# Dealing a graph layer's projections out between its neighbour sums

## The chip, the core and the metric

The kernel runs on one NeuronCore of a Trainium2 chip. The core has five engines with instruction queues of their own, each worked off in order: TensorE (PE, matmuls; PEld its weight loads), VectorE (DVE), ScalarE (ACT), GpSimd (POOL) and SyncE (SP, which here only issues transfers). Matmuls write to PSUM, a small memory of eight banks. The metric is device microseconds of one execution; the time before is the median of three runs.

## The reference

A graph of 6250 nodes with 256 features and 100,000 edges, sorted by their target node, each edge with one of 8 relations. Two relational graph layers run after a layer norm, then a layer norm and a mixture of 8 experts of which each node takes two. Cut to what matters:

```python
def _rgcn_conv(x, W, Wroot, b, src, dst, etype):
    seg = dst * R + etype
    sums = segment_sum(x[src], seg)              # per node and relation
    cnt = segment_sum(ones, seg)
    mean = (sums / maximum(cnt, 1)).reshape(N, R, -1)
    return x @ Wroot + b + einsum('nrd,rde->ne', mean, W)

h = relu(_rgcn_conv(layernorm(x), W1, Wroot1, b1, ...))
x = x + _rgcn_conv(h, W2, Wroot2, b2, ...)
# experts: logits = xf @ Wg + bg; the two largest, softmax;
# out += w[e] * (gelu(xf @ W1[e] + b1[e]) @ W2[e] + b2[e]); x = x + out
```

## The kernel before

Edges come in 782 tiles of 128. A tile's source rows are fetched by one indirect gather on POOL (L680) from the table `xs`, which holds each row as three bf16 parts; DVE builds a one-hot tile `oh` of target and relation (L686); TensorE multiplies the two, 2 chunks by 3 parts, into a PSUM tile of sums `pg` (L696), and in layer 1 adds a matmul with `ones16` that counts the edges (L699). There are 13 buffers `ge` for gathered tiles.

`_plan` puts the tiles into 194 groups of 1 to 6. Each group has one `pg` tile of which there are two; ACT zeroes it ahead of the sums (L672, in `tiles_in`) and DVE adds it into one of two rings in SBUF at an offset read from a register (L710, in `add`). Groups are walked from both ends of the sorted edges, "up" and "down", one ring for each; the two meet in one block (`join`).

Nodes come in 49 blocks of 128. A block is *whole* at the step after which no further group adds to it; `_plan` works that step out from a margin over the expected edge positions. From there its work is due at fixed distances in steps: `counts`, `invert` (1 / count), `project`, `clear`, `finish`, `turn`, `logits`. `project` makes the block's output: the root term and 8 relations, 2 chunks each, 18 fp32 matmuls in five PSUM tiles `pr` of two terms each (L783), which DVE scales by the inverse counts and adds up in `h` (L791, L793). `clear` zeroes the block's ring rows on ACT (L800). `finish` writes the block out: in layer 1 as three bf16 parts to the table of layer 2, in layer 2 to the output and, normalised, to `xnd`. `turn` transposes it on TensorE, and `logits` makes the gating logits of layer 2 and, once four blocks have them, calls `choose` (the two experts of each node, with a PSUM tile `rpp`); `append` writes the lists of nodes by expert (PSUM tile `rpl`).

In PSUM, `pg` has three banks a tile in layer 1 and two in layer 2. `pr`, the transposes, the counts and the logits share two tiles under the tag "mm"; choosing and lists have two of their own in layer 2 under the tag "rt".

The order within an engine is not the order of the program text: a planner places the instructions by priority and its own estimate of when each is ready, so text that is next to each other may come out mixed. Bounds worked out by `_plan` are tested against the data in the kernel; if one failed, a slower general arm would run.

After the layers the experts run in tiles of 256 rows: gather, two fp32 matmul stages, and a scatter that adds to the output.

Of the kernel before, what the change touches and what calls it, by code (L numbers as in the profile page):

```python
# [48 lines left out]
P = 128  # L49
# [45 lines left out]
Z = 4.8  # L95
WIN = 64
RB = 3
READ = 2
TAKE = 3
EARLY = 30  # L100

# [1 line left out]
def _plan(N, E, R):  # L103

    T = -(-E // P)

    def windows(ts, n):

        mid = n // 2
        lo, hi = [0] * n, [-(1 << 30)] * n
        for t in ts:
            for k in range(n + 1):
                i0, i1 = t * P, max(0, t + k - mid) * P
                mean = N * (i1 * i1 - i0 * i0) / (E * E)
                sd = 2 * N * i0 / (E * E) * math.sqrt(abs(i1 - i0)) + 0.004 * abs(mean)
                if k < n:
                    lo[k] = min(lo[k] if t != ts[0] else 1 << 30, math.floor(mean - Z * sd) - (k < mid))
                if k:  # L120
                    hi[k - 1] = max(hi[k - 1], math.ceil(mean + Z * sd) + (1 if k <= mid else 2))
        shift = -min(lo)
        w = [(a + shift, b + shift) for a, b in zip(lo, hi)]
        return shift, w, max(b for _, b in w)


    NB = -(-N // P)
    mid = max(0, round((N / 4 - P / 2) / P))
    split = round(T * math.sqrt((mid + 0.5) * P / N))
    regions = []  # L130
    t = 0
    while t < T:
        left = (split if t < split else T) - t
        for n in range(min(6, left), 0, -1):
            ng = max(1, min(36, left) // n)
            shift, w, width = windows((t + n // 2, t + n * (ng - 1) + n // 2), n)
            if width <= WIN:
                break
        regions.append((t, n, ng, shift, w, width))
        t += n * ng  # L140
    groups = []
    for r, (t0, n, ng, *_) in enumerate(regions):
        for g in range(ng):
            groups.append((t0 + g * n, n, r))
    NG = len(groups)
    up = [g for g in range(NG) if groups[g][0] < split]
    down = list(range(NG - 1, len(up) - 1, -1))
    size = [sum(groups[g][1] for g in s) for s in (up, down)]
    seq, at, n = [], [0, 0], [0, 0]
    while len(seq) < NG:  # L150

        s = int(n[1] * (size[0] - EARLY) < n[0] * size[1])
        if at[s] == len((up, down)[s]):
            s = 1 - s
        g = (up, down)[s][at[s]]
        seq.append(g)
        at[s] += 1
        n[s] += groups[g][1]
    step = {g: q for q, g in enumerate(seq)}

    whole = []
    for b in range(NB):
        if b == mid:
            whole.append(NG - 1)
            continue
        p = math.sqrt((b + 1 if b < mid else b) * P / N)
        dev = Z * math.sqrt(E * p * (1 - p)) + 1
        t = int(min(E - 1, E * p + dev) // P) if b < mid else int((E * p - dev) // P)
        whole.append(step[next(g for g, (t0, n, _) in enumerate(groups) if t0 + n > t)])


    bounds = []
    for g in range(NG):
        read, taken = ([b for b in range(NB) if whole[b] + n < step[g]] for n in (READ - 1, TAKE))
        if g < len(up):
            bounds.append((sum(b < mid for b in read) or -NB, sum(b < mid for b in taken) + RB))
        else:
            n = sum(b > mid for b in read)
            bounds.append((NB - sum(b > mid for b in taken) - RB, NB - n if n else 2 * NB))
    return T, regions, groups, seq, len(up), mid, whole, bounds  # L180
# [3 lines left out]
def kernel(  # L184
# [451 lines left out]
    with tc.If(go == 1) as cmp:  # L636
        with ExitStack() as arm:
# [18 lines left out]
            def layer(k):  # L656
# [10 lines left out]

                def tiles_in(g):
                    t0, n, r = groups[g]
                    pg = psum.tile([P, nd, R, WIN], F32, name="pg", tag="pg", bufs=2)  # L670
                    wd = regions[r][5]
                    state["zeroed"] = nc.scalar.copy(pg[:, :nd, :, :wd],  # L672
                                                     zeros[:, None, None, :wd].to_broadcast([P, nd, R, wd]))
                    got = []
                    ohs = ap.tile([P, OHW], BF16, name="oh", bufs=3)
                    o0 = 0
                    for t in range(t0, t0 + n):
                        m = P if t < EC else ER
                        ge = ap.tile([P, 3, KD, P], BF16, name="ge", bufs=13)
                        nc.gpsimd.indirect_dma_start(  # L680
                            out=ge[:m].rearrange("p s k d -> p (s k d)"), out_offset=None, in_=xs[k][:, :],
                            in_offset=bass.IndirectOffsetOnAxis(ap=idx[:m, t : t + 1], axis=0))
                        a, b = regions[r][4][t - t0]
                        oh = ohs[:m, o0 : o0 + (b - a) * R].rearrange("p (r d) -> p r d", r=R)
                        o0 += (b - a) * R
                        nc.vector.tensor_scalar(oh, iota16[:m].rearrange("p (r d) -> p r d", r=R)[:, :, a:b],  # L686
                                                rel[:m, t : t + 1], None, op0=OP.is_equal)
                        got.append((ge, oh, m, a, b))
                    state[g] = (pg, got)

                def sums(g):
                    pg, got = state[g]
                    for ge, oh, m, a, b in got:
                        for c in range(KD):
                            for s in range(3):
                                nc.tensor.matmul(pg[:, c, :, a:b], ge[:m, s, c, :], oh, start=False, stop=False,  # L696
                                                 skip_group_check=True)
                        if nd > KD:
                            nc.tensor.matmul(pg[:, KD, :, a:b], ones16[:m], oh, start=False, stop=False,  # L699
                                             skip_group_check=True)  # L700

                def add(g):
                    pg, _ = state.pop(g)
# [59 lines left out]
                def invert(b):  # L763
                    if k == 0:
# [2 lines left out]
                        nc.vector.tensor_scalar(invs[:, b], pc[:, :R], 1.0, None, op0=OP.max)  # L767
                        nc.vector.reciprocal(invs[:, b], invs[:, b])

                def project(b):  # L770

                    n = rows(b)
# [3 lines left out]
                    h = ap.tile([P, D], F32, name="h", bufs=2)  # L776
                    lhs = [(R, [xT[:, c, :n] for c in range(KD)])]
                    lhs += [(r, [ring[:, c, r, s0 : s0 + n] for c in range(KD)]) for r in range(R)]
                    for i in range(0, R + 1, 2):
                        pr = psum.tile([P, 2, D], F32, name="pr", tag="mm", bufs=MM)  # L780
                        for j, (r, chunks) in enumerate(lhs[i : i + 2]):
                            for c in range(KD):
# [5 lines left out]
                        for j, (r, _) in enumerate(lhs[i : i + 2]):  # L788
                            if r == R:
                                extra = bias1 if k == 0 else state.pop(("xb", b))  # L790
                                nc.vector.tensor_tensor(h[:n], pr[:n, j], extra[:n], OP.add)  # L791
                            else:
                                nc.vector.scalar_tensor_tensor(h[:n], pr[:n, j], invs[:n, b, r : r + 1], h[:n],  # L793
                                                               op0=OP.mult, op1=OP.add)
                    state["h", b] = h

                def clear(b):
# [37 lines left out]
                def logits(b):  # L835
                    if k == 1:
                        gate(place[b], state.pop(("t", b)), rows(b))
                        for o, bs in batches[:-1]:
                            if b == bs[-1]:
                                while todo and todo[0][-1] is not todo[-1][-1]:  # L840
                                    batch()
                                c = choose(bs, o, ap, "rt", 2)
                                todo.extend((j, i, False, c) for j, i in enumerate(bs))

                tiles_in(seq[0])
                due = {}
                for b, q in enumerate(whole):
                    for d, f in ((-1, root), (0, counts), (1, invert), (2, project), (2, clear), (2, finish), (3, turn), (4, logits)):
                        due.setdefault(q + d, []).append((f, b))

                todo = []
# [1 line left out]
                def batch():  # L853

                    if todo:
                        append(*todo.pop(0), ap, "rt", 2)

                due.setdefault(joined, []).append((join, mid))

# [3 lines left out]
                            f(b)  # L863

                cleared[:] = [[(-1, ins) for _, ins in c] for c in cleared]
                for q in range(NG + 5):
                    if k == 1 and q == 2:

                        with tc.issue_after(state["zeroed"].ins):
# [4 lines left out]
                    if q == 0 and k == 0:  # L874
                        for c in range(KD + 1):
                            nc.vector.memset(rings[0][:, c], 0.0)
                            nc.scalar.copy(rings[1][:, c], zeros[:, None, 0:1].to_broadcast([P, R, RING + WIN]))
                    run(q, project, clear)
                    run(q, turn)
                    run(q, finish)  # L880
                    if q < NG:
                        sums(seq[q])
                    run(q, invert, logits)
                    if q < NG:
                        add(seq[q])
# [388 lines left out]
```

## Time and profile before

| | us |
|---|---|
| median of three runs | 3025.12 (3022.4 to 3025.45) |
| profiled execution | 3826.98 |
| its span | 3825.1 |
| TensorE busy, mean granted clock | 2804.2, 0.844 |
| POOL, DVE, ACT busy | 1800.2, 1621.8, 1023.8 |
| gathers L680 | 1564 of 966 ns, first at 83.6, last at 2953.1 |
| sums L696, counts L699, projections L783 | 9384, 782, 3528 matmuls |

The profile is of one execution of its own, which here takes 802 us longer than the median of the runs. A line of a group of instructions has the source line, the engine, the operation and the tiles it writes and reads; after a bar its busy time, the mean duration of one and the idle time of the engine just before, with what ended it. In a line of the timeline the first number is the start, the second the duration, and the bracket holds the idle time before and what ended it. A line of waits gives the total, how often, and the longest. "issue" is idle time that ends with nothing which the profile shows.

### The profile page before, as it was taken

To read this page: it belongs to the slowest core of one execution; us is meant where nothing else is said; L and a number is where in the kernel's file an instruction comes from. 1 tells how busy PE (TensorE), PEld (TensorE's weight loads), DVE (VectorE), ACT (ScalarE), POOL (GpSimd) and SP (SyncE) were. 2 spreads that over 40 slices of the span, in tenths; PEclk is the share of its full clock that TensorE was granted. 3 is DMA by queue.
4 is the path that set the end of the run, shared out by engine and by line. 5 is a ranking of instruction groups with operands and counts; after the bars stand their busy time and mean duration, and the time that the engine had idled before them with its cause. 6 is when DMAs were issued, how large, how long until landed. Compare 5 with 4: busy or idle time off the path is not lost.

```text
span 3825.1 us, 52037 instructions
## 1 busy us (share of the span) xinstructions
PE 2804.2 (73%) x18131; PEld 2321.9 (61%) x18131; DVE 1621.8 (42%) x4676; ACT 1023.8 (27%) x1378; POOL 1800.2 (47%) x2109
## 2 busy tenths in 40 slices
PE   5566676766666876566667766776777499999998
PEld 2455565555555655455555655555555388888887
DVE  6444454544444545344554445544445311111111
ACT  6223233322222323122222222221222122222221
POOL 2545555555555554455555555555444033333332
PEclk8678897878888878677888878787878699999999
DMA  6344444444444443444444444444344444344442
GB/s 226 112 116 117 127 127 119 128 118 117 117 119 118 115 117 105 130 121 126 124 127 120 122 126 131 125 124 123 112 116 116 153 119 115 101 115 115 108 112 45
DMA packets 215591, 461.05 MB, mean 121 GB/s; under 512 B 50716, under 2 KB 123222, under 8 KB 215190
## 3 DMA queue, kind: packets, MB, share of 16 engines
q0 software_dynamic: 120384, 334.45, 32.9%
q1 hardware_dynamic: 83724, 112.33, 8.8%
q10 hardware_dynamic: 11210, 10.81, 0.9%
q8 instruction: 149, 2.44, 0.3%
q14 instruction: 124, 1.02, 0.1%
HBM read 412.02 MB, written 46.31 MB: 120 GB/s over the span
## 4 chain that ended last, share of the span: by engine, by line
PE 59%; issue 12%; another core or an unknown queue 11%; DVE 9%; ACT 5%; DMA 3%; POOL 1%; SPq 0%; DVEq 0%; ACTq 0%; POOLq 0%
PE pr L783 21%; PE pg L696 14%; PE ph L1214 10%; PE po L1225 9%; DVE ring L710 3%; ACT pg L672 2%; DVE oh L686 1%; DVE h L793 1%; ACT ring L800 1%; PE pg L699 1%; PE pl L323 1%; POOL ge L680 1%; PE pt L314 1%; DMA ge<-xs,idx 1%
## 5 line engine op out<-in xcount | busy, mean ns | idle before, releaser
L680 POOL DMA_INDIRECT ge<-xs,idx x1564 | 1511.2, 966 | 1425.1 <-PE pg L696 746.8
L696 PE MATMUL pg<-oh,ge 128*128 128x200 bf16 (+24 forms) x9384 | 932.0, 257 | 441.0 <-issue 207.7
L696 PEld LDWEIGHTS <-ge 128*128 128x128 bf16 x9384 | 764.3, 113 | 578.5 <-issue 508.5
L783 PE MATMUL pr<-gw,ring 128*128 128x256 f32 (+1 forms) x3136 | 861.3, 430 | 222.0 <-DVE h L793 104.6
L783 PEld LDWEIGHTS pr<-gw,ring 128*128 128x128 f32 (+1 forms) x3136 | 663.2, 217 | 382.1 <-DVE h L793 126.3
L710 DVE TENSOR_TENSOR ring<-pg,ring 128x1176 f32 (+31 forms) x388 | 457.0, 1178 | 846.1 <-remote 270.6
L672 ACT COPY pg<-zeros 128x1176 f32<-128x1176 f32 (+31 forms) x388 | 380.4, 981 | 981.4 <-DVE ring L710 584.3
L793 DVE SCALAR_TENSOR_TENSOR h<-pr,invs,h 128x256 f32<-128x256 f32 (+1 forms) x784 | 376.9, 481 | 245.3 <-PE pr L783 178.4
L800 ACT COPY ring<-zeros 128x3072 f32<-128x3072 f32 (+1 forms) x98 | 227.8, 2324 | 794.1 <-PE pr L783 674.3
L1214 PE MATMUL ph<-xT,w 128*128 128x256 f32 x1696 | 377.0, 381 | 0.0
L1225 PE MATMUL po<-fw,hT 128*128 x1696 | 374.4, 379 | 0.0
L1225 PEld LDWEIGHTS po<-fw,hT 128*128 128x128 f32 x1696 | 322.2, 190 | 43.8
L1214 PEld LDWEIGHTS ph<-xT,w 128*128 128x128 f32 x1696 | 320.1, 191 | 41.9
L686 DVE TENSOR_SCALAR oh<-iota,rel 128x152 bf16<-128x152 f16 (+25 forms) x1564 | 331.9, 270 | 30.9 <-PE pg L699 16.2
L1215 ACT ACTIVATE hT<-ph,bcol 128x256 f32<-128x256 f32 x424 | 200.4, 473 | 534.6 <-PE ph L1214 534.2
L1230 POOL DMA_INDIRECT out_dram<-fo,ti x106 | 168.7, 1591 | 229.9 <-DVE wt L1199 107.3
L1186 POOL DMA_INDIRECT xg<-xnd,ti x106 | 105.5, 995 | 357.4 <-DMA ti<-tlist 242.3
L699 PE MATMUL pg<-oh,ones 128*128 128x128 bf16 (+24 forms) x782 | 200.2, 256 | 14.2 <-issue 14.1
L1228 DVE TENSOR_TENSOR fo<-po,b2b 128x256 f32<-128x256 f32 x106 | 45.0, 425 | 299.5 <-PE po L1225 291.6
L1209 DVE COPY bcol<-b1c 128x8 f32 x53 | 9.0, 171 | 302.4 <-ACT hT L1215 301.9
L316 ACT COPY tT<-pt 128x256 f32<-128x256 f32 (+1 forms) x98 | 36.2, 370 | 297.9 <-remote 208.6
L699 PEld LDWEIGHTS <-ones 128*128 128x128 bf16 x782 | 87.8, 112 | 23.5 <-issue 19.9
(190 smaller groups left out, 1431.4 us busy)
## 6 DMA issues: line engine op xcount, KB each, us to landing
w<-in_L_ffn_W_dram SPq DMA_DIRECT2D x53, 1024.0 KB
ge<-xs,idx POOLq DMA_INDIRECT x1564
xt<-in_x_dram SPq DMA_DIRECT2D x96, 128.0 KB
xs<-xb SPq DMA_DIRECT2D x8, 1152.0 KB
xs<-hb SPq DMA_DIRECT2D x48, 192.0 KB
fw<-in_L_ffn_W_dram ACTq DMA_DIRECT2D x8, 1024.0 KB
xt<-in_x_dram SPq DMA_DIRECT2D x8, 768.0 KB
out_dram<-h SPq DMA_DIRECT2D x48, 128.0 KB
```

The costliest lines, as they stand in the source:

```text
L672: state["zeroed"] = nc.scalar.copy(pg[:, :nd, :, :wd], zeros[:, None, None, :wd].to_broadcast([P, nd, R, wd]))
L680: nc.gpsimd.indirect_dma_start(out=ge[:m].rearrange("p s k d -> p (s k d)"), out_offset=None, in_=xs[k][:, :], in_offset=bass.IndirectOffs ...
L686: nc.vector.tensor_scalar(oh, iota16[:m].rearrange("p (r d) -> p r d", r=R)[:, :, a:b], rel[:m, t : t + 1], None, op0=OP.is_equal)
L696: nc.tensor.matmul(pg[:, c, :, a:b], ge[:m, s, c, :], oh, start=False, stop=False, skip_group_check=True)
L699: nc.tensor.matmul(pg[:, KD, :, a:b], ones16[:m], oh, start=False, stop=False, skip_group_check=True)
L710: a = nc.vector.tensor_tensor(slot, pg[:, :nd, :, :wd], slot, OP.add).ins
L783: mm = nc.tensor.matmul(pr[:n, j], chunks[c], w[:, c, r, :], start=(c == 0), stop=(c == KD - 1))
L793: nc.vector.scalar_tensor_tensor(h[:n], pr[:n, j], invs[:n, b, r : r + 1], h[:n], op0=OP.mult, op1=OP.add)
L800: ins = nc.scalar.copy(at, zeros[:, None, None, 0:1].to_broadcast([P, nd, R, P]))
L1214: nc.tensor.matmul(ph[:, :TK], w1[:, k, h * P : (h + 1) * P], xT[:, k, :], start=(k == 0), stop=(k == KD - 1))
L1215: nc.scalar.activation(hT[:, h, :], ph[:, :TK], AF.Gelu, bias=bcol[:, h : h + 1], scale=1.0)
L1225: nc.tensor.matmul(po[:, :D], hT[:, k, f * P : (f + 1) * P], rhs, start=(k == 0), stop=(k == KH - 1))
```

## The change

`project` no longer emits its matmuls at once: it appends its five pairs to a list, and `sums` takes one pair from it after each tile; what is left is emitted after the group's sums and before its `add`. Within a step, `turn` and `clear` come first, then `finish`, then `project`. `clear`, `finish`, `turn` and `logits` are due one step later than before. In layer 2 the sums have three PSUM tiles, and choosing and lists take theirs from "mm". The count matmul loads one column of ones in place of 128 and writes one row. In `_plan`, the margin of a block grows from 1 edge to 32 (`P / 4`) and the groups that may run while a block is read are fewer (`READ - 1`, that is 1, becomes 0). That moves two of the 49 blocks by one step each (from step 164 to 165 and from 28 to 29) and changes 21 of the 194 groups' bounds.

```diff
-        dev = Z * math.sqrt(E * p * (1 - p)) + 1
+        dev = Z * math.sqrt(E * p * (1 - p)) + P / 4
...
-        read, taken = ([b for b in range(NB) if whole[b] + n < step[g]] for n in (READ - 1, TAKE))
+        read, taken = ([b for b in range(NB) if whole[b] + n < step[g]] for n in (0, TAKE))
...
-                    pg = psum.tile([P, nd, R, WIN], F32, name="pg", tag="pg", bufs=2)
+                    pg = psum.tile([P, nd, R, WIN], F32, name="pg", tag="pg", bufs=2 + k)
...
-                            nc.tensor.matmul(pg[:, KD, :, a:b], ones16[:m], oh, start=False, stop=False,
+                            nc.tensor.matmul(pg[0:1, KD, :, a:b], ones16[:m, 0:1], oh, start=False, stop=False,
                                              skip_group_check=True)
+                        go_on()
...
+                pairs = []
+
+                def go_on():
+
+                    if pairs:
+                        f, i = pairs.pop(0)
+                        f(i)
+
                 def project(b):
...
-                    for i in range(0, R + 1, 2):
+                    def pair(i):
                         pr = psum.tile([P, 2, D], F32, name="pr", tag="mm", bufs=MM)
...
+                    pairs.extend((pair, i) for i in range(0, R + 1, 2))
                     state["h", b] = h
...
-                                c = choose(bs, o, ap, "rt", 2)
+                                c = choose(bs, o, ap, "mm", 2)
...
-                    for d, f in ((-1, root), (0, counts), (1, invert), (2, project), (2, clear), (2, finish), (3, turn), (4, logits)):
+                    for d, f in ((-1, root), (0, counts), (1, invert), (2, project), (3, clear), (3, finish), (4, turn), (5, logits)):
...
-                        append(*todo.pop(0), ap, "rt", 2)
+                        append(*todo.pop(0), ap, "mm", 2)
...
-                for q in range(NG + 5):
+                for q in range(NG + 6):
...
-                    run(q, project, clear)
-                    run(q, turn)
+                    run(q, turn, clear)
                     run(q, finish)
+                    run(q, project)
                     if q < NG:
                         sums(seq[q])
+                    while pairs:
+                        go_on()
                     run(q, invert, logits)
```

More of the change, by code (lines that the diff above doesn't have):

```diff
@@ L97 @@
 RB = 3
-READ = 2
 TAKE = 3
```

## The prediction

> **What bounds the kernel now.** I first cut the profiled execution into its stages, from start to end: preparation, gathers of layer 1, the turn between the layers, gathers of layer 2, the turn to the experts, the experts.
>
> ```profile
> core 0: us, PE busy (x) PEld busy (x) DVE busy (x) ACT busy (x) POOL busy (x), PEclk, DMA share, GB/s
> 0.00:84.00 84.00, 45.03 (x132) 19.55 (x132) 55.01 (x223) 52.62 (x82) 15.31 (x334) 0.91 0.73 238
> 84.00:1508.00 1424.00, 973.24 (x7303) 802.57 (x7304) 697.67 (x1647) 439.49 (x474) 759.44 (x782) 0.81 0.42 119
> 1508.00:1555.00 47.00, 34.19 (x186) 27.82 (x184) 26.85 (x61) 14.02 (x18) 0.98 (x2) 0.88 0.12 37
> 1555.00:2953.00 1398.00, 953.32 (x6695) 774.38 (x6695) 667.25 (x2170) 301.25 (x361) 749.44 (x781) 0.80 0.44 125
> 2953.00:3057.00 104.00, 47.44 (x247) 36.77 (x248) 39.55 (x166) 17.55 (x24) 8.50 (x9) 0.70 0.42 141
> 3057.00:3826.00 769.00, 750.98 (x3572) 660.83 (x3570) 135.42 (x412) 198.84 (x420) 266.56 (x204) 0.99 0.41 104
> ```
>
> The experts are TensorE alone (751 of 769 us at clock 0.99) and no line of theirs changes. The change lives in the two layers, where no engine is full: TensorE 68% in both, POOL 53%. So I read the timeline at one projection.
>
> ```profile
> 2509.11 6.27 PE L783 MATMUL pr<-gw,ring 128*128 128x256 f32 x20 [2.21 <-DVE h L793]
> 2515.89 3.47 PE L696 MATMUL pg<-oh,ge 128*128 128x208 bf16 x52
> 2516.51 0.95 POOL L680 DMA_INDIRECT ge<-xs,idx  x1 [9.49 <-PE pg L696]
> 2517.76 0.94 POOL L680 DMA_INDIRECT ge<-xs,idx  x1 [0.30 <-issue]
> 2519.01 0.95 POOL L680 DMA_INDIRECT ge<-xs,idx  x1 [0.30 <-PE pg L696]
> ```
>
> Two things are to be seen. Free of waits, gathers start 1.25 us apart (2516.51, 2517.76, 2519.01: 0.95 of work, 0.30 of gap). And a projection in one piece holds TensorE long enough that no gathered tile (13 buffers) is released: POOL stands 9.49 us, then the sums catch up.
>
> The first gives a floor: 782 gathers by 1.25 us is 977 us a layer. The profiled layers take 1424 and 1398, that is 447 + 421 = 868 us above it. The median of the runs shown is 3025.1, against 3827.0 for the profiled execution (span 3825.1 and 1.9 around it). Taking the other stages as profiled (84 + 47 + 104 + 769 + 1.9 = 1006), the runs leave 2019 us for both layers, only 64 above two floors. So nearly all the 868 belongs to the profiled execution, or the floor is lower in runs than I can see. This decides the size of any gain.
>
> Who holds the gathers? Summing POOL's gaps beyond the usual 0.30 us gives 884 us; in 552 of them, TensorE was in a projection (472) or waiting to start one (80): 62%, or 5.6 us for each of 98 blocks. TensorE's own waits (total, times, longest), first two lines layer 1, last two layer 2:
>
> ```profile
> PE pg L696 <- ACT pg L672: 130.4, 49, 15.1
> PE pr L783 <- DVE h L793: 42.2, 18, 5.7
> PE pr L783 <- DVE h L793: 63.0, 26, 8.3
> PE pg L696 <- ACT pg L672: 36.8, 19, 5.2
> ```
>
> **The change, part by part, against 3827.0.**
>
> *Dealing out.* The planner orders the instructions itself, so I compared the two orders. A projection is 18 matmuls (9 terms by 2 chunks; each shows as two in the trace) in five pieces. Blocks whose 18 stand in one run: layer 1 from 23 to 7 of 49, layer 2 from 19 to 21. So many were already dealt by the planner, and net only 14 blocks are newly dealt. TensorE's work is the same; gathered tiles are released earlier. Bound: nothing, to 14 x 9.5 = 133 us (the stand above). I take half of the mean 5.6 us: 14 x 2.8 = -40, since what TensorE owes is still owed. The wait for DVE's h falls with the same blocks: (42.2 + 63.0) x 14/42 = -35 (0 to -105). The wait for invs (54.7 in layer 1) I leave: in both orders the transpose of the counts stands right before the first piece and shares its tiles.
>
> Against it speaks a rule. The rows first, two chains of projections in layer 1 and one of the experts:
>
> ```profile
> 657.80 6.11 PE pr L783 x28
> 756.20 6.50 PE pr L783 x16
> 3082.42 6.91 PE ph L1214 x32
> ```
>
> That is 0.218, 0.406 and 0.216 us each: full and half clock, and the layers' means are 0.81 and 0.80. The Trainium skill (TensorE: Matmul & The Clock Gate, "A second HAM failure mode: psum-queue depth-cycling") says that small idle times between groups which cycle through PSUM make the clock fall back and recover again and again. By the rule, a dense projection cut into pieces would run at half clock: 14 blocks x 36 x 0.19 = +96 us. By the row of POOL's gaps, TensorE is behind when a projection is due, so sums fill the places between pieces and nothing idles: 0. I take 0, and keep +96 as the end.
>
> *Third tile of sums in layer 2.* ACT zeroes a tile when the add two steps earlier has read it; with three tiles it is an add three steps earlier. TensorE's wait there is 36.8 us; I take -30 (0 to -37). Layer 1, with 130.4, keeps two tiles.
>
> *Gating and lists on the projection's tiles.* In layer 2 the two "rt" tiles go. A pair that meets one tile taken waits for two h (2 x 0.48 us). In the new order 2 of 12 choices are closely followed by pieces, and 17 of 48 lists. A choice holds its tile 8.8 us (median, first matmul to last reading). 2 x 8.8 + 17 x 0.97 = 34 at most, 0 at least since the old order also has pieces among lists; I take +15.
>
> *Later steps.* finish, turn, logits and clear come one step later. DMAs and counts of instructions are the same: per block one row of xs or two of out and xnd on SP's queue, not moved past a gather, as POOL has its own queue. Inside a layer the following groups' gathers hide it (5 us of POOL per step of four tiles). At a layer's end, one more block's chain may stand after the last sum: +2 each, +4 (0 to +12). clear on ACT (1.9 and 2.75 us) frees ring rows for adds two steps after the projection, now with one step between; behind it in ACT's queue wait the next zeroing and DVE's add. The order has two zeroed tiles ahead of it in 33 of 49 blocks of layer 1 (31 before), so 0; without that cover 49 x 2.75 = 135 us of TensorE's waits.
>
> *The rest.* The count matmul with one weight column: 782 at the pace of their columns either way (the trace's one-column matmuls of 32 columns start 0.025 us apart, no slower than their neighbours), weight load hidden: 0, at most the whole 88 us of loads if the cover were real work. The plan: two blocks become whole one step later, and the stricter bounds still hold (worked out from the inputs, the least margin is 20 rows, 42 before), so the same arm runs: 0.
>
> Sum: -40 - 35 - 30 + 15 + 4 = -86, so 3741 profiled. For the runs there are two scalings. In proportion, 86/868 of 64 gives -6. Unscaled gives -86, which is more than the 64 that stand above the floor. Waits by order exist in runs too, but count only where gathers run dry; I take a third of the unscaled, -30: **2995**.
>
> **The rivals.**
> - *Hidden anyway.* Gathers pace the runs, and the 13 buffers (16 us of gathers) cover a projection of 8 us at full clock. For it: the 64 us. Time: 3019 to 3031.
> - *More than that.* If a gather's period without the profiler is under 1.25 us, the floor is lower and TensorE's waits count in full: -86 and more, 2940. Against it: the period is sharp, 1.245 to 1.251 us in over half of all gathers.
> - *Slower: the shared tiles.* In layer 2 a list's tile is held 10.9 us (median) in the old order. If the new order keeps that, 48 x 10.9 = 523 of 1398 us leave pairs one tile: 37% of 245 pairs, 92, each 0.97 to 1.5 us: +90 to +138 on TensorE. It decides when TensorE's work and waits pass 977 us: with the profiled busy time of 953 spare is 24, so +66 to +114 and some 3110; at full clock (I work out 655 us from columns and 0.216) spare is 322 and it costs nothing. Between: 3060. Against it: in the new order only 3 matmuls of projections stand between the two matmuls of a list (6 before).
> - *Slower: the clock*, by the rule above: half of +96 reaches the runs, 3073.
>
> **How the numbers follow.** The forecast 0.45, more 0.10, hidden 0.15, shared tiles 0.15, clock and what I don't see 0.15. About 0.2%, 6 us, is what a measurement can tell from no change; the forecast's own range is 2960 to 3018, all of it faster. So faster 0.55, within 0.2% 0.15, slower 0.30. The range takes in most of "more" and the slower cases up to 3060: 2935 to 3060.
>
> **What would show it.** Right: POOL's idle time before gathers falls, its part on projections most; waits of pr for h fall to about 70 us; layer 2's wait of pg for the zeroing nearly gone; granted clock in the layers not under 0.80. Wrong: the clock falls; pr waits for lists' or choices' readers in layer 2; sums of layer 1 wait longer than 130 us for ACT; the turns longer than 47 and 104 us. The likeliest error is the scale from the profiled execution to the runs.

## The result, and the profile after

The changed kernel takes 3221.23 us (median of 4 runs, 3218.32 to 3226.95); the kernel before, beside it, 3023.76 (3021.12 to 3025.45). The ratio is 1.0656, 95% interval 1.0638 to 1.0675: 197 us slower. The forecast was 2995, the range ended at 3060, so the sign was wrong.

To read the numbers one thing has to be known: on some chips the kernel before takes 3.80 to 3.83 ms in every run, on others 3.02, and the first profile (3827 us) came from the one kind and the timed runs from the other; so below, a kernel is compared only with the kernel before on its own chip. The kernel before was profiled again on the 3.02 ms chip. These are its two layers with the turn between them and the turn to the experts:

```profile
core 0: us, PE busy (x) PEld busy (x) DVE busy (x) ACT busy (x) POOL busy (x), PEclk, DMA share, GB/s
...
82.00:1127.00 1045.00, 866.32 (x7405) 743.18 (x7405) 709.15 (x1677) 441.70 (x484) 767.12 (x782) 0.91 0.57 164
1127.00:1169.00 42.00, 24.09 (x124) 18.69 (x124) 17.07 (x40) 8.93 (x11) 8.78 (x10) 0.76 0.18 51
1169.00:2150.00 981.00, 826.78 (x6658) 687.53 (x6659) 666.09 (x2169) 300.84 (x362) 740.66 (x769) 0.91 0.62 176
2150.00:2234.00 84.00, 39.93 (x220) 30.74 (x220) 38.48 (x159) 13.51 (x17) 10.10 (x11) 0.70 0.35 112
```

And the same of the changed kernel, in the same columns (span 3224.8):

```profile
82.00:1151.00 1069.00, 968.37 (x7312) 722.05 (x7313) 702.13 (x1653) 436.89 (x476) 764.32 (x781) 0.93 0.56 159
1151.00:1199.00 48.00, 34.21 (x177) 26.49 (x175) 23.52 (x54) 13.61 (x18) 1.08 (x2) 0.83 0.25 79
1199.00:2326.00 1127.00, 882.52 (x6686) 712.53 (x6686) 665.25 (x2153) 292.00 (x359) 752.37 (x782) 0.83 0.55 153
2326.00:2441.00 115.00, 57.58 (x232) 43.73 (x233) 45.42 (x177) 16.99 (x20) 6.42 (x7) 0.66 0.24 79
```

Three rows carry the loss. Layer 1 is 24 us longer by these windows, and TensorE is busy 102 us more in it with no more matmuls. Layer 2 is some 130 us longer at a lower clock; its row of before leaves out 13 of the 782 gathers, so the two rows differ by more. The turn to the experts is 31 us longer. The same cut made at the gathers themselves, for every kernel run on this chip, is the table of this section (in us; a layer goes from the start of its first gather to the start of its last, and the turn to the experts ends with their first matmul; "stalls" are POOL's gaps between gathers beyond the usual 0.30 us, summed where the gap is over 0.8):

| kernel | layer 1 | turn | layer 2 | turn to experts | stalls, layer 1 / 2 |
|---|---|---|---|---|---|
| before | 1036.7 | 38.3 | 997.2 | 78.2 | 31.9 / 6.3 |
| changed, run again | 1064.6 | 46.9 | 1127.2 | 112.9 | 61.8 / 136.0 |
| before, count matmul with one column | 1071.1 | 38.8 | 1000.8 | 77.6 | 67.0 / 8.9 |
| dealing out, later steps and plan alone | 1028.3 | 37.5 | 997.5 | 85.4 | 27.8 / 4.4 |
| before, with all the sharing | 1043.4 | 42.7 | 1145.0 | 99.2 | 36.8 / 155.9 |
| before, lists alone share | 1040.0 | 38.3 | 1130.3 | 93.4 | 34.2 / 140.4 |
| changed, list's tile copied at once | 1067.8 | 47.0 | 1057.5 | 96.2 | 67.9 / 66.2 |
| dealing out, all share four tiles | 1023.1 | 39.8 | 1055.3 | 88.9 | 24.1 / 64.7 |

In both layers the time lost is the time by which the gathers stand longer: 27.9 against 29.9 in layer 1, 130.0 against 129.7 in layer 2. The loss of layer 2 comes in a few long stands. This is the changed kernel's timeline at one of them:

```profile
1332.65 3.12 SPq L422 DMA_DIRECT2D tlist<-rids  x8
...
1335.82 0.36 SPq L405 DMA_DIRECT2D xnd<-rwd  x1
...
1337.83 0.28 DVE L414 TENSOR_SCALAR rids<-rpl 8x128 int32<-8x128 f32 x1 [3.33 <-DMA xnd<-rwd]
1338.15 0.28 DVE L415 SCALAR_TENSOR_TENSOR rids<-rpl,rids 8x128 int32<-8x128 f32 x1
...
1338.45 3.04 SPq L422 DMA_DIRECT2D tlist<-rids  x8
...
1338.48 2.08 PE L791 MATMUL pr<-gw,hTs 128*128 128x256 f32 x4 [4.43 <-DVE rids L415]
...
1343.16 0.27 DVE L414 TENSOR_SCALAR rids<-rpl 8x128 int32<-8x128 f32 x1
...
1343.30 7.97 PE L791 MATMUL pr<-gw,ring 128*128 128x256 f32 x28 [1.04 <-DVE h L801]
...
1352.36 1.90 ACT L809 COPY ring<-zeros 128x2048 f32<-128x2048 f32 x1 [28.59 <-DVE ring L710]
...
1356.18 0.37 PE L695 MATMUL pg<-oh,ge 128*128 128x56 bf16 x4 [4.40 <-ACT pg L671]
...
1357.64 0.94 POOL L679 DMA_INDIRECT ge<-xs,idx  x1 [17.18 <-PE pg L695]
```

The projection's first pair waits 4.43 us until DVE has read a list out of its PSUM tile (L415). DVE itself stood 3.33 us before that reading: L414 writes the one `rids` buffer, which the eight row transfers of the list before, issued from 1332.65, still read (the row names `xnd<-rwd`, a transfer issued right behind them, which doesn't touch that buffer). DVE reads the next list 5.3 us later (1337.83 to 1343.16), after the eight transfers from 1338.45; no two lists of this profile are read at a shorter distance. Then 28 matmuls stand in one run, ACT clears ring rows, the sums wait 4.40 us for a zeroed tile, and POOL has stood for 17.18 us. A projection in one run is what the change was to end. TensorE's waits in layer 2 (total, times, longest) show how little of this is under the name of the list:

```profile
PE pg L695 <- DMA ge<-xs,idx: 143.7, 186, 9.7
PE pg L695 <- ACT pg L671: 43.8, 22, 5.2
PE pr L791 <- DVE rids L415: 14.0, 6, 4.4
```

The 143.7 us of waits for gathers don't name a cause of their own (the kernel before has 124.3 there): after a stand of the gathers, sums wait for data. Only six waits for a list are left to be seen, 14.0 us together.

### The profile page after: what moved, and what is told of

The parts are those of the page before. It is cut to its first block, busy times and chain, and to the rows that moved or that the text cites. A ratio compares the mean times of both kernels' runs of the same rounds, so it can differ in the third digit from the quotient of the medians.

```text
span 3224.8 us, 52110 instructions
## 1 busy us (share of the span) xinstructions
PE 2743.6 (85%) x18131; PEld 2190.8 (68%) x18131; DVE 1627.6 (50%) x4676; ACT 1013.4 (31%) x1378; POOL 1807.8 (56%) x2110
## 5 line engine op out<-in xcount | busy, mean ns | idle before, releaser
L695 PEld LDWEIGHTS <-ge 128*128 128x128 bf16 x9384 | 681.1, 107 | 465.9 <-DMA ge<-xs,idx 237.9
L791 PE MATMUL pr<-gw,ring 128*128 128x256 f32 (+1 forms) x3136 | 774.0, 398 | 14.8 <-DVE h L801 14.7
L791 PEld LDWEIGHTS pr<-gw,ring 128*128 128x128 f32 (+1 forms) x3136 | 609.0, 199 | 115.5 <-DVE h L801 24.9
L710 DVE TENSOR_TENSOR ring<-pg,ring 128x1464 f32 (+28 forms) x388 | 456.7, 1177 | 283.4 <-PE pg L695 128.4
L685 DVE TENSOR_SCALAR oh<-iota,rel 128x152 bf16<-128x152 f16 (+25 forms) x1564 | 337.3, 273 | 46.9 <-PE pg L695 24.2
L698 PE MATMUL pg<-oh,ones 128*1 128x128 bf16 (+24 forms) x782 | 179.9, 230 | 0.0
L698 PEld LDWEIGHTS <-ones 128*1 128x1 bf16 x782 | 61.9, 79 | 105.5 <-issue 57.7
L791 PE MATMUL pr<-gw,hTs 128*128 128x256 f32 (+1 forms) x196 | 73.0, 506 | 18.6 <-DVE rids L415 14.9
```

The costliest lines, as they stand in the source:

```text
L698: nc.tensor.matmul(pg[0:1, KD, :, a:b], ones16[:m, 0:1], oh, start=False, stop=False, skip_group_check=True)
L710: a = nc.vector.tensor_tensor(slot, pg[:, :nd, :, :wd], slot, OP.add).ins
L791: mm = nc.tensor.matmul(pr[:n, j], chunks[c], w[:, c, r, :], start=(c == 0), stop=(c == KD - 1))
```

## The experiments

Ratios are to the kernel before on the same chip and at the same time, with 95% intervals.

### The kernels themselves again

Before, run again for its profile:

> The kernel before, unchanged, for a second profile. If the 802 us between its first profiled execution and its runs belong to that one execution, this profile shows a span near 3023 us, gathers of both layers together near 2019 us (64 us above two floors of 977), and gather starts 1.25 us apart where nothing waits. If the profile always slows this kernel, the span is near 3825 again.

> The kernel before once more, for a profile from a chip on which it takes about 3024 us (should the chip be one with 3834, it only repeats the last such profile). From the variants: layer 1's gathers 1040 to 1046 us as in b_share (which leaves layer 1 alone), the turn about 43, layer 2 about 985 (8 above its floor of 977), the turn to the experts 80 to 95.

> The kernel before once more, for a profile from a chip on which it takes about 3024 us; the last three profiles of it all came from chips with 3830. From the variants: layer 1's gathers 1040 to 1046 us, the turn about 43, layer 2 about 985, the turn to the experts 80 to 95.

Measured: 3835.58, 3838.07 and 3021.38 us. The first two came from chips of the 3.83 ms kind, on which engines show idle time that no event of the trace ends (TensorE 379 and 369 us of it, and 346 in the first profile; in the third profile it has none). The third is the profile of before used above. The changed kernel on the 3.02 ms chip:

> The changed kernel, unchanged, beside the same runs of the kernel before as the three that follow. The four runs so far came from a chip on which the kernel before takes 3834 us instead of 3024. There the changed kernel should lie near its variant with the wide count matmul (3873), as the one-column count matmul made no difference (1.0006). On a chip with 3024 us, 3221.

Measured: 3221.59, ratio 1.0647 (1.0620 to 1.0674). The loss repeats, stage by stage.

### The count matmul with one column

```diff
-                            nc.tensor.matmul(pg[:, KD, :, a:b], ones16[:m], oh, start=False, stop=False,
+                            nc.tensor.matmul(pg[0:1, KD, :, a:b], ones16[:m, 0:1], oh, start=False, stop=False,
```

That alone in the kernel before, on three chips:

> The kernel before with the one-column count matmul alone. Theory 'weights': in the trace of the changed kernel a count matmul starts about 95 ns later than its columns ask (185 against 90 ns at 200 columns), and so does the sums matmul after it: 782 x 0.19 = 147 us of TensorE in layer 1; part of it falls into TensorE's spare time, so 3085 to 3135 us. Theory 'order' (the loss comes from dealing out and the later steps): within 6 us of 3024.

> The kernel before with the one-column count matmul alone, on a chip with 3024 us. 'Weights': of 147 us of TensorE in layer 1 what the spare time leaves: layer 1's gathers take 1070 to 1100 us instead of 1043, 3050 to 3085. If TensorE's spare time takes it all: within 6 us of 3024. It also shows whether the pause is there: starts 185 instead of 90 ns apart at 200 columns on both sides of the count matmul.

> The kernel before with the one-column count matmul alone. On chips with 3834 us it made no difference (1.0006, 1.0011) though the pauses were there (185 instead of 90 ns). On a chip with 3024 us: layer 1's gathers 1070 to 1100 instead of 1043, 3050 to 3085. If the spare time takes it all: within 6 us of 3024.

Measured: 3842.82, ratio 1.0006 (0.9991 to 1.0022); 3838.11, 1.0011 (0.9994 to 1.0029); and on the 3.02 ms chip 3055.58, 1.011 (1.009 to 1.0129). So no cost is seen where the gathers stand anyway, and 33 to 36 us where they don't. Its layer 1, by the same windows:

```profile
82.00:1153.00 1071.00, 971.02 (x7332) 726.64 (x7333) 707.69 (x1661) 440.62 (x476) 764.44 (x781) 0.93 0.55 159
```

TensorE's 866 us are 971, as in the changed kernel. Where they come from is seen in the timeline at full clock. First the kernel before, tiles of 176 columns:

```profile
458.57 0.62 PE L696 MATMUL pg<-oh,ge 128*128 128x176 bf16 x6
459.02 0.24 PE L699 MATMUL pg<-oh,ones 128*128 128x176 bf16 x1
459.10 0.66 PE L696 MATMUL pg<-oh,ge 128*128 128x176 bf16 x6
```

Then the changed kernel:

```profile
505.02 0.63 PE L695 MATMUL pg<-oh,ge 128*128 128x176 bf16 x6
505.58 0.24 PE L698 MATMUL pg<-oh,ones 128*1 128x176 bf16 x1
505.75 0.67 PE L695 MATMUL pg<-oh,ge 128*128 128x176 bf16 x6
```

Read the starts, not the durations. From six sums to the count it was 0.45 us and is 0.56; from the count to the next sums it was 0.08 and is 0.17. Over all tiles of 200 columns the two spacings (last sum to count, count to next sum) go from 90 and 90 ns to 185 and 184, with 80 columns from 36 and 36 to 131 and 131: about 95 ns on each side with either width. 782 x 0.19 is 149 us of TensorE's time, of which 105 show as busy time in the row of layer 1. Where the weight loads stand shows more. The load of the ones, and the page's group of these loads, before:

```profile
458.95 0.10 PEld L699 LDWEIGHTS <-ones 128*128 128x128 bf16 x1
...
L699 PEld LDWEIGHTS <-ones 128*128 128x128 bf16 x782 | 83.4, 107 | 2.9
```

and in the changed kernel:

```profile
505.58 0.08 PEld L698 LDWEIGHTS <-ones 128*1 128x1 bf16 x1
...
L698 PEld LDWEIGHTS <-ones 128*1 128x1 bf16 x782 | 61.9, 79 | 105.5 <-issue 57.7
```

With 128 columns the load begins 0.07 us ahead of its matmul (458.95, 459.02), while the sum before it is still running; the idle time ahead of all these loads is 2.9 us. With one column the load and its matmul begin together (505.58), and so do the wide load and the sum behind them (in the trace 505.75 each); the idle time is 105.5 us. So neither load goes ahead of its matmul, under the one that runs, as the 128-column loads do. The Trainium skill (TensorE: Matmul & The Clock Gate, "LDWEIGHTS (loading the stationary operand)") has the load's time go by its columns, 1.2 a ns. The 107 ns for 128 agree; for one column it would make 1 ns (an estimate), and the row has 79 and a stop on both sides, so the measurement decides. The same page ("Weight-path perf modes — Fast Weight Load (FWL) and DoubleRow") says that a fast load of weights is on only for 128 columns that are not fp32. That fits, but whether it is the cause no run here shows: widths between 1 and 128 weren't run.

The changed kernel with the 128-column matmul back:

> The changed kernel with the 128-column count matmul back. 'weights': 60 to 110 us faster than 3221, so 3110 to 3160, and layer 1's gathers end under 1010 us after they begin (1070 in the changed kernel). 'order': 3215 to 3227.

Measured on a 3.83 ms chip: 3873.11, 1.0071 (1.0045 to 1.0098). There the rest of the change is a small loss: the two parts below, -3.3% and +4.1% on this kind of chip, nearly cancel.

### Dealing out alone

The changed kernel with 128 columns, tiles of their own for choosing and lists, and two tiles of sums:

```diff
-                    pg = psum.tile([P, nd, R, WIN], F32, name="pg", tag="pg", bufs=2 + k)
+                    pg = psum.tile([P, nd, R, WIN], F32, name="pg", tag="pg", bufs=2)
...
-                            nc.tensor.matmul(pg[0:1, KD, :, a:b], ones16[:m, 0:1], oh, start=False, stop=False,
+                            nc.tensor.matmul(pg[:, KD, :, a:b], ones16[:m], oh, start=False, stop=False,
...
-                                c = choose(bs, o, ap, "mm", 2)
+                                c = choose(bs, o, ap, "rt", 2)
...
-                        append(*todo.pop(0), ap, "mm", 2)
+                        append(*todo.pop(0), ap, "rt", 2)
```

> The changed kernel with the 128-column count matmul and with the PSUM tiles of before (two of sums, own tiles for choosing and lists): dealing out, later steps and the plan are left of the change. Theory 'weights and shared tiles': at least as fast as the kernel before: 2970 to 3030 on a chip with 3024 us; 3700 to 3720 with 3834. Theory 'order': slower than before, 3150 to 3220 on a chip with 3024.

Measured: 3011.97, 0.9958 (0.9941 to 0.9976): 0.4% under the kernel before and 6.5% under the changed one. Its two layers:

```profile
82.00:1110.00 1028.00, 849.52 (x7342) 729.67 (x7343) 699.96 (x1660) 433.44 (x476) 761.54 (x781) 0.92 0.59 165
1148.00:2145.00 997.00, 830.25 (x6722) 684.99 (x6723) 662.46 (x2171) 297.91 (x364) 754.62 (x781) 0.91 0.63 175
```

Layer 1 gains 8 us and layer 2 nothing: at 997 us it was already 20 above the 977 of the gathers' period, which is 1.25 us here too. The turn to the experts takes 7 of the 8 back, and the two profiled executions (3019.35 and 3021.38) differ by 2 us; so in which stage the 13 us between the medians arise isn't shown. The clock is no lower than before (0.92 and 0.91).

The same with the one-column count matmul left in, on a 3.83 ms chip:

> The changed kernel with two tiles of sums in layer 2 and own PSUM tiles for choosing and lists, as before. Theory 'shared tiles': in the changed kernel two lists that wait for their predecessor's transfer hold both tiles, a projection waits up to 4.4 us for DVE rids and then goes with one tile; gathers then stand 5 to 17 us, 97 us in all in layer 2: 3110 to 3150. 'order': 3215 to 3227, or slower since the third tile of sums is gone.

Measured: 3715.82, 0.967 (0.9638 to 0.9702): 118 us gained, nine times as much. There the gathers of the kernel before stand for 440 and 408 us in the two layers (profile of 3835.58, same chip), and with this edit for 380 and 334.

The version without sharing, with the logits one step earlier:

```diff
-                    for d, f in ((-1, root), (0, counts), (1, invert), (2, project), (3, clear), (3, finish), (4, turn), (5, logits)):
+                    for d, f in ((-1, root), (0, counts), (1, invert), (2, project), (3, clear), (3, finish), (4, turn), (4, logits)):
```

> The changed kernel with 128-column count matmul, with tiles of their own for choosing and lists and two tiles of sums, and now with the logits back at four steps after a block is whole, in the turn's step (five in the change). Theory (the turn to the experts is longer by 7 us since one more step's chain stands behind the last gather): 3 to 7 us less than with five steps, so 0.993 to 0.996 of the kernel before, and the turn to the experts at 78 to 83 us. Rival (the logits then hold TensorE for a root not yet there, in front of sums): 0 to 15 us more than with five steps, 0.996 to 1.001.

Measured on a chip with 3798.49 for the kernel before: 3673.29, 0.9674 (0.9650 to 0.9699). Its turn to the experts is 86.0 us, 93.7 in the run above with five steps; but the whole is not told apart from that run's 0.967, and it wasn't run on the 3.02 ms chip, for which the expected ratio was meant. So the step's price is seen in one stage of one profile each, and no gain of the whole is shown.

### Sharing the projection's tiles

All the sharing in the kernel before, with the third tile of sums, and then with two tiles of sums:

```diff
-                    pg = psum.tile([P, nd, R, WIN], F32, name="pg", tag="pg", bufs=2)
+                    pg = psum.tile([P, nd, R, WIN], F32, name="pg", tag="pg", bufs=2 + k)
...
-                                c = choose(bs, o, ap, "rt", 2)
+                                c = choose(bs, o, ap, "mm", 2)
...
-                        append(*todo.pop(0), ap, "rt", 2)
+                        append(*todo.pop(0), ap, "mm", 2)
```

> The kernel before with the PSUM tiles of the change alone (three tiles of sums in layer 2, choosing and lists on the projection's tiles). 'Shared tiles': slower than before by 70 to 120 us on a chip with 3024 us, by 80 to 160 on one with 3834. If sharing only hurts with the new order, within 15 us of before, or faster by the third tile of sums (up to 37 us).

> The kernel before with choosing and lists on the projection's tiles, but two tiles of sums (two PSUM banks of layer 2 stay empty). If the third tile of sums helps, this is slower than b_share (3196) by up to 37 us; if the third tile is worth nothing, within 10 us of 3196. If the third tile itself were the cause of the loss, within 20 us of 3024.

Measured: 3195.63, 1.0552 (1.0514 to 1.0590) on the 3.02 ms chip; with two tiles of sums 3996.58, 1.0405 (1.0373 to 1.0437) on a 3.83 ms chip, 165 us there. The 170 us are more than the 70 to 120 expected. It is the sharing, without any dealing out; the third tile isn't needed for the loss, but with the two runs on different chips its own share is not shown. Then the lists alone (the last pair of lines), and the choosing alone (the pair before it):

> The kernel before with the lists alone on the projection's tiles; choosing keeps its own, and there are two tiles of sums. If the lists' wait for the transfer is the cause, most of b_share's loss is here: 100 to 170 us slower than before, on either kind of chip. If choosing is the cause: within 30 us of before.

> The kernel before, with the choosing of layer 2 alone on the projection's tiles; its lists keep tiles of their own. Theory (the lists, paced by their transfers, hold the shared tiles and put projections late): 12 choices of some 9 us stand against 48 lists, so at most 30 us over the kernel before, and the projections' first pieces stand near as soon after their blocks as before. Rival (any further user of these tiles delays the projections, by the order alone): half or more of what the lists cost, 80 us and up. Layer 2's gathers: 1000 to 1025 us by the theory, 1060 and more by the rival (on a chip that runs the kernel before in about 3020 us).

Measured: lists 3178.09, 1.0525 (1.0504 to 1.0545), on the 3.02 ms chip; choosing 3843.84 beside 3798.49, 1.0123 (1.0091 to 1.0154), on a 3.80 ms chip. The lists alone cost 158 of the 170 us. Choosing costs 45 us on its chip, more than the 30 expected and about half of what the rival asked; what it would cost on the other chip is open. With lists alone, TensorE's and DVE's waits in layer 2:

```profile
PE pr L783 <- DVE rids L416: 29.2, 6, 5.3
...
PE rpl L411 <- DVE rids L416: 15.0, 5, 4.2
```

```profile
DVE rids L415 <- PE rpl L411: 31.6, 9, 6.2
DVE rids L415 <- DMA tlist<-rids: 25.9, 9, 5.1
```

A pair waits for DVE's reading of a list, and DVE waits for the transfer of the list before it. In the kernel before that second wait shows once, with 4.4 us, and what it holds up then are the lists' own tiles.

### Held tiles, or a late order?

Sharing can cost in two ways: a list holds a tile for its transfer, or the planner, handing out tiles of one name in turn, puts projections behind the lists. Two kernels tell them apart. The changed kernel with the list copied to SBUF as soon as TensorE is done, so that the tile no longer waits for a transfer:

```diff
+        got = pool.tile([X, P], F32, name="rgot", bufs=1 if last else 2)
+        nc.vector.tensor_copy(got, pl[:X, :P])
...
-        nc.vector.tensor_scalar(t[:, :P], pl[:X, :P], 0.0, float(N + 1 - b * P), op0=OP.is_equal, op1=OP.mult)
-        nc.vector.scalar_tensor_tensor(t[:, :P], pl[:X, :P], float(b * P - 1), t[:, :P], op0=OP.add, op1=OP.add)
+        nc.vector.tensor_scalar(t[:, :P], got, 0.0, float(N + 1 - b * P), op0=OP.is_equal, op1=OP.mult)
+        nc.vector.scalar_tensor_tensor(t[:, :P], got, float(b * P - 1), t[:, :P], op0=OP.add, op1=OP.add)
```

> The changed kernel in which a list's PSUM tile is copied to SBUF first (one more DVE operation of about 0.27 us for each of 49 lists), so that it does not hold the projection's tile while it waits for the transfer of the list before. 'Shared tiles': gains most of what own tiles gained, 60 to 100 us against the changed kernel on a chip with 3024 us, 100 to 150 on one with 3834. If the tile is not what is waited for (but DVE, which waits in order for the transfer), no gain: within 15 us of the changed kernel.

Measured: 3129.23, 1.0340 (1.0312 to 1.0368), 92 us under the changed kernel beside it, and no wait of `pr` for a list is left. The order of the instructions hardly explains this gain: projections stand about as late in it as in the changed kernel (counts below). And the version of dealing out alone, in which everything in layer 2 that is not a sum shares one set of four tiles:

```diff
+            TR = MM = 2 + 2 * k
...
-                                c = choose(bs, o, ap, "rt", 2)
+                                c = choose(bs, o, ap, "mm", MM)
...
-                        append(*todo.pop(0), ap, "rt", 2)
+                        append(*todo.pop(0), ap, "mm", MM)
```

> Dealing out with the wide count matmul, two tiles of sums, and in layer 2 one set of four PSUM tiles for projections, choosing and lists together. 'Shared tiles' says that it is not the sharing but the number that hurts: two lists leave two tiles for pairs, so 2995 to 3015 on a chip with 3024 us (dealing out with own tiles: 3012). If sharing as such hurts (the order of requests), 3050 or more.

> Dealing out with the wide count matmul and one set of four PSUM tiles for projections, choosing and lists in layer 2. On a chip with 3831 us it took 3742 (0.976). On a chip with 3024: 2995 to 3015 if the number of tiles is what counts, 3050 or more if sharing as such hurts.

Measured: 3741.88, 0.9761 (0.9737 to 0.9786), on a 3.83 ms chip, where dealing out alone has 0.967; and 3079.21, 1.0197 (1.0177 to 1.0216), on the 3.02 ms chip, where it has 0.9958. With four tiles nothing waits for a tile, and still 72 us are lost. Its timeline, TensorE and then POOL:

```profile
1476.59 7.07 PE L791 MATMUL pr<-gw,ring 128*128 128x256 f32 x32
...
1490.90 7.07 PE L791 MATMUL pr<-gw,ring 128*128 128x256 f32 x32
...
1499.11 6.21 PE L791 MATMUL pr<-gw,ring 128*128 128x256 f32 x28
```

```profile
1492.26 0.94 POOL L679 DMA_INDIRECT ge<-xs,idx  x1 [0.30 <-PE pr L791]
1505.79 0.94 POOL L679 DMA_INDIRECT ge<-xs,idx  x1 [12.59 <-PE pg L695]
```

Three blocks' projections stand close together, with 25 matmuls of sums between the first two, and the gathers stand 12.59 us. That is the order. It can be counted in TensorE's instructions: how many tiles of sums stand between the step at which a block is whole and the first piece of its projection in layer 2 (the third column is the number within which 90% of the blocks stay):

| kernel | median | 90% within |
|---|---|---|
| before | 3.0 | 7.2 |
| dealing out alone | 6.0 | 8.6 |
| changed | 7.0 | 21.9 |
| changed, list's tile copied at once | 7.0 | 21.0 |
| before, lists alone share | 6.0 | 18.2 |
| before, choosing alone shares | 4.2 | 10.1 |
| before, all share, two tiles of sums | 6.0 | 17.2 |
| before, all share, three tiles of sums | 11.2 | 24.0 |
| dealing out, all share four tiles | 6.0 | 17.2 |

Wherever lists share, the late tail is over twice that of before. So the loss by sharing, some 170 us, is about half tiles held by transfers (92 by the copy, which leaves the order about as late) and half a late order (72 by the four tiles, with which nothing waits for a tile). That the planner's turn of tiles makes the order late is argued from these counts; a kernel with the old order forced on shared tiles wasn't run. Nor was one with more `rids` buffers, for the lists' transfers have to stay in order.

## Why the prediction was wrong

The parts measured one by one multiply to the whole: on the 3.02 ms chip 0.9958 x 1.011 x 1.0552 = 1.0623 against 1.0647 (on the other kind 0.967 x 1.0405 = 1.0062 against 1.0071 with 128 columns). In us: -13 + 34 + 167 = +188 against +196.

- *"Gating and lists on the projection's tiles"*, the step that failed: +15, at most 34, measured +167 (with the third tile of sums; the lists alone +158). I counted 17 lists that hold a pair up for two of DVE's h, 0.97 us each. A list's tile waits for a transfer, at least 5.3 us from list to list and four lists in a row; and I compared the orders only for what stands between lists and pieces, not for how late the pieces stand behind their blocks.
- *The rival "Slower: the shared tiles"* had the mechanism, at 0.15. Its size, +66 to +114, was too small, and its point of decision was wrong: it let pairs be delayed so long as TensorE has spare time in the layer as a whole. By that rule sharing would have cost nothing on the timed chip: over all gathers of layer 2 TensorE is busy 835 us in the kernel before, and with +90 to +138 that stays under 977. In the changed kernel it is busy 883 of 1127 us of layer 2, so it has time to spare and the loss is there all the same. What decides is one burst: 13 gathered tiles cover 16 us, and a held tile, a projection in one run and a clearing in a row take more. The argument held against it, 3 matmuls in place of 6 between a list's two, looked at the wrong end: the hold comes after the second matmul, until DVE reads.
- *"The rest": the count matmul at 0*, measured +33 to +36. The cover was not real, as the bound of 88 us allowed, but it isn't the loads' own 88 us that come out: it is two stops of 95 ns. I took one-column matmuls that follow one another (0.025 us). The right row was in the first profile too: in choosing, where matmuls have 32 moving columns or fewer, one with a single weight column starts 98 to 145 ns (median 110) after the one with 128 ahead of it, and those with a single one follow one another at 25 ns.
- *Dealing out, -40, and the wait for h, -35; a third of it for the runs.* On the 3.02 ms chip dealing out, later steps and plan together have -13. The reading that the runs stand 64 us above two floors was nearly right: 60 in layer 1 and 20 in layer 2 are 80. "Hidden anyway" was therefore nearly right for this part. On the kind of chip of the first profile even the unscaled -40 - 35 + 4 = -71 was too small: -118.
- *The clock, taken 0:* right for dealing out (0.92 and 0.91 in its two layers). In layer 2 of the changed kernel it fell to 0.83, and on this chip it is 0.82 to 0.86 in every kernel that shares. TensorE's busy time there grew by some 50 us (835 to 883, both over all 782 gathers), an estimate of the most that the clock took itself; it wasn't separated from the stands that go with it.
- *Third tile of sums, -30:* not seen. In the profile of before on the timed chip the wait that it was to end is 14.2 us in layer 2, so no more was there. In the changed kernel, with three tiles, it is 43.8, but with the lists alone on shared tiles and two tiles of sums it is 46.9: it goes with the sharing, not with the third tile. The third tile was never run alone; beside sharing it comes with a later order (11.2 tiles against 6.0 in the table).
- *Later steps, +4:* the turn to the experts has +7 with dealing out alone. In the whole it has +35; sharing adds 21 of it, 15 with the lists alone, and 7 stay open, as do 4 of the 9 us of the turn between the layers.
- *The signs to look for* were in part right ones: waits of `pr` for lists' readers in layer 2 are there, and both turns are longer than before on the timed chip (47 against 38 us, 113 against 78). The waits of layer 1's sums for ACT and a clock under 0.80 didn't come (57.1 us; 0.93 and 0.83).
- *The range* ended at 3060 because +15 had 34 as its upper end. A bound worked out from how long DVE reads left out what DVE waits for.

## What to carry to other kernels

Before two uses share a set of PSUM tiles, ask what the slowest reader of each waits for, and count how late the planned order puts the urgent one; a transfer behind a reader in a tile's life can cost more than its waits show (14.0 us here under the name of the lists, in a layer that lost 130), because the waits that are seen afterwards are others'. A narrower weight load need not be a cheaper one: look for a place in the trace where a wide load meets a narrow one, and read the spacing of the starts. If the profiled execution is far from the median, have the kernel before profiled where it is timed, before any waits are priced; idle time of TensorE that nothing ends was a mark of it here (346 us in the first profile, none on the timed chip).

## What was not expected of the hardware

- A one-column weight load among 128-column ones stops TensorE for about 95 ns before and after it (185 in place of 90 ns from start to start with 200 columns at full clock, 131 in place of 36 with 80 columns).
- The same kernel takes 3020 to 3026 us on one chip and 3798, 3831 and 3834 on three others, run for run, with the same period of gathers (1.25 us) and the same time in the experts. The difference lies in the two layers; there the granted clock is 0.79 to 0.81 in place of 0.91, and TensorE alone has 346 to 379 us of idle time that the trace puts down to nothing, in place of none. What it is wasn't found; dealing out is worth 3.3% on the one kind and 0.4% on the other, and the one-column count matmul, which costs 1.1% on the one, can't be measured on the other.
